# Softmax sums of two attention layers: turned and added up by VectorE, quadrants summed by 16-column products

## The chip, the cores and the metric

One Trainium2 chip, one core of it. The time is the device time of one execution in microseconds (us), given as the median of several executions. Everything is float32; TensorE multiplies it in two passes per product, except where operands are declared float32r ("fp32r"), which takes one.

## The reference

Two residual layers over x of shape (8, 32, 32, 512): a batch of 8 images, 1024 positions each (32 x 32), 512 channels. gn is a group norm over 32 groups of channels without weights.

```python
# layer 0: 16 heads of 32
q, k, v = split(gn(x) @ w_qkv)                 # w_qkv 512 x 1536
attn = softmax(q @ k.T * 32 ** -0.5)           # per image and head 1024 x 1024
x = x + (attn @ v) @ w_proj + b_proj
# layer 1: 4 heads of 128, with logits of relative position
q, k, v = gn(x) @ Wq * 128 ** -0.5, gn(x) @ Wk, gn(x) @ Wv
attn = softmax(q @ k.T + rel_w(q) + rel_h(q))
x = x + (attn @ v) @ Wo
```

A softmax is an exponential divided by the sum of the exponentials over the 1024 keys. How that sum is formed is what the change is about: 8 images x 16 heads x 1024 queries of them in layer 0, 8 x 4 x 1024 in layer 1.

## The kernel before

**Layout.** The program is unrolled over the 8 images ("batches"). Activations lie transposed, channels on the 128 partitions, positions along the row. Attention computes the transposed scores: 128 keys on the partitions, 512 queries along the row, so a query's sum runs over the partitions and over 8 key blocks. No maximum is subtracted; every sum is instead checked (L665 writes the maximum of sum + 1/sum), and at the end one product with ones (L1296) carries the verdict to a flag, on which the general path would run instead. It does not run here.

**Projections.** Each of the eight (512 x 512 matrices) is done in halves of seven products of half-size blocks, from sums of input blocks (forming, L343, additions at L370, written f_xn, f_ao and so on) and prepared sums of weights. `by_columns` (L327) issues a product as four 32-column strips (L331). Seven (about L407) takes three banks of PSUM, x, y and z, from `bank`, a pool of three 2 KB banks under one tag, and VectorE adds up y and p1 into snapshots a (L421) and b (L429), each before TensorE may go on adding to y. The name says which projection: y_wo and a_wo belong to the output projection of layer 1, y_q to a query projection.

**Attention of layer 0** (`attention_0`, from L685): 64 steps a batch over (m, h, j): m is one of 4 groups of four heads, h one of 2 halves of the queries, j one of 8 key blocks. A group is the 8 steps of one (m, h), so there are 8 groups a batch. `front` (L690): products of keys and queries into the four-bank tile ps (L698, eight products of 64 keys per step), one exponential over 128 x 2048 (L713) into one of three buffers of e_room. `back`, for the step before: value products into the bank "acc" (L724), and VectorE's addition of the exponentials into the group's sum esum, 128 x 2048 (L736, seven a group). At a group's last step ScalarE copies acc into q (L739), the undivided output. `finish`, called before the next step's front: four products with a 128 x 32 block of ones and esum, one per head, into the same bank "acc" (L746): each head's 32 partitions then hold its sums, repeated. `normalise` (L651): a copy to SBUF by ScalarE (L657), a 32 x 32 block transpose by VectorE (L659), so that 16 columns hold the sums once, reciprocal (L662), check (L665), transpose back with broadcast (L675), multiplication into q by GpSimd (POOL, L679).

**Attention of layer 1** (`attention_1`, from L811): 4 heads x 2 halves x 8 key blocks, again 64 steps and 8 groups a batch. `front`: keys and queries (L821), position logits (L822) into a bank, exponential of 128 x 512 (L824). `back`: value products (L833), VectorE's additions into es (L842, L844), a copy (L847). `finish` is a generator, of which a part runs per step: esum is split into its fp32r part (cast by ScalarE, L861) and the rest (subtraction on VectorE, L863), two steps later two one-pass products with 128 x 128 ones (L869, L870) go into a bank of ps, then normalise. Only three groups of the last batch (`beside`), which run next to first-layer attention, use one fp32 product with ones (L854) into `bank` instead. The very last group has VectorE do the final multiplication.

**What sets the order.** `side_by_side` (L1138) interleaves the 64 steps of attention_0 of batch b with everything else that is ready: output projection of layer 0 of batch b-1 (after_0), output projection of layer 1 of batch b-2 with its output transposes (after_1, put_out, L1098) and the group norm of batch b-1 (group_norm, L265; norm_1), then second (query, key, value projections of layer 1 and position logits, posT, L802, L807), attention_1, and the projections of batch b+1. Each part yields its cost; attention_1 yields 0 in all but the last batch, so it runs as one block of about 125 us in each period of about 470 us, and attention_0 of the batch stands still in that time. Within that program order a scheduler places each engine's instructions by its own estimate; `issue_after` and `keep_in_program_order` are further constraints. Each engine then runs its own queue in order; semaphores between the queues are the only other order.

Of the kernel before, what the change touches and what calls it, by code (L numbers as in the profile page):

```python
# [9 lines left out]
F32 = mybir.dt.float32  # L10
# [17 lines left out]
def quick_path(  # L28
# [52 lines left out]
    def bank(name, shape=None):  # L81
        return psum.tile(shape or [P, NB], F32, tag="bank", name=name, bufs=3)
# [1 line left out]

    ident = consts.tile([P, P], F32, tag="ident", name="ident")
    make_identity(nc, ident)
    ones_r = consts.tile([P, P], F32R, tag="ones", name="ones")
    nc.gpsimd.memset(ones_r.bitcast(F32), 1.0)
    ones = ones_r.bitcast(F32)
    bproj_sb = consts.tile([P, CC], F32, tag="bproj_sb", name="bproj_sb")  # L90
    with nc.allow_non_contiguous_dma(reason="512 values, once"):
        nc.gpsimd.dma_start(bproj_sb, b_proj.rearrange("(cc p) -> p cc", p=P))
# [5 lines left out]
    neg_half = consts.tile([P, CC], F32, tag="neg_half", name="neg_half")  # L98
    nc.gpsimd.memset(neg_half, -0.5)


    sel = consts.tile([P, IH, IW], F32R, tag="sel", name="sel")

    def fill_sel():
        for u in range(4):
            rows = slice(32 * u, 32 * u + 32)
            eye = ident[rows, rows]
            eye = eye.unsqueeze(2) if u % 2 else eye.unsqueeze(1)
            nc.vector.tensor_copy(sel[rows], eye.to_broadcast([32, IH, IW]))
# [541 lines left out]
    def normalise(dst, acc_sums, name, engine=nc.gpsimd):  # L651

        su = mem.tile([P, NB], F32, tag="rec", name=f"su_{name}", bufs=2)
        nc.scalar.copy(su, acc_sums)  # L657
        turned = mem.tile([P, NB], F32, tag="rec", name=f"tu_{name}", bufs=2)
        nc.vector.transpose(turned, su)  # L659
        few = turned.rearrange("p (t c) -> p t c", c=32)[:, :, 0]  # L660
        rec = mem.tile([P, NB // 32], F32, tag="few", name=f"rc_{name}", bufs=2)
        nc.vector.reciprocal(rec, few)  # L662
        at = check_at[0]
        check_at[0] += 1
        nc.vector.tensor_tensor_reduce(  # L665
            out=few,
            in0=few,
            in1=rec,
            op0=ALU.add,
            op1=ALU.max,  # L670
            scale=1.0,
            scalar=0.0,
            accum_out=checks[:, at : at + 1],
        )
        nc.vector.transpose(  # L675
            su.rearrange("p (t c) -> p t c", c=32),
            rec.unsqueeze(2).to_broadcast([P, NB // 32, 32]),
        )
        engine.tensor_tensor(dst, dst, su, op=ALU.mult)  # L679
# [5 lines left out]
    def attention_0(q, k, v, b, blocks=range(NT)):  # L685
# [55 lines left out]

        def finish(m, h, esum):
            name = f"0_{b}_{m}_{h}"
            su = psum.tile([P, NB], F32, tag="acc", name=f"sums_{name}", bufs=1)
            for r in range(HB):
                nc.tensor.matmul(  # L746
                    su[r * D0 : (r + 1) * D0, :],
                    ones[:, :D0],
                    esum[:, r, :],
                    start=True,  # L750
                    stop=True,
                )
            normalise(q[m][:, h * NB : (h + 1) * NB], su, name)

        pending = None
        for at in steps:
            if "ended" in state:
                finish(*state.pop("ended"))
            e = front(*at)
            if pending is not None:  # L760
                back(*pending)
            pending = (*at, e)
            yield 2
        back(*pending)
        yield 1
        finish(*state.pop("ended"))

    def position_logits(q, posT, b):

# [41 lines left out]
    def attention_1(q, k, v, posT, b, beside=0):  # L811
# [37 lines left out]

        def finish(h, c, esum):  # L850
            name = f"1_{b}_{h}_{c}"
            if (h * NH + c + 1) * NT < beside:
                su = bank(f"sums_{name}")
                nc.tensor.matmul(su, ones, esum, start=True, stop=True)  # L854
                normalise(q[:, h, c * NB : (c + 1) * NB], su, name)
                return

            yield

            greater = mem.tile([P, NB], F32R, tag="rec", name=f"sg_{name}", bufs=2)  # L860
            nc.scalar.copy(greater, esum)  # L861
            rest = mem.tile([P, NB], F32R, tag="rec", name=f"sr_{name}", bufs=2)
            nc.vector.tensor_sub(rest, esum, greater.bitcast(F32))  # L863

            yield
            yield

            su = psum.tile([P, HB, NB], F32, tag="ps", name=f"sums_{name}", bufs=1)[:, 0, :]
            nc.tensor.matmul(su, ones_r, greater, start=True, stop=False)  # L869
            nc.tensor.matmul(su, ones_r, rest, start=False, stop=True)  # L870

            end = (b, h, c) == (B - 1, H1 - 1, NH - 1)
            normalise(
                q[:, h, c * NB : (c + 1) * NB], su, name, nc.vector if end else nc.gpsimd
            )

# [257 lines left out]
    def run(part):  # L1134
        for _ in part:
            pass
# [65 lines left out]
    WV0.add_up([nc.gpsimd] * 2 + [nc.vector] * 2, nc.gpsimd, keep=True)  # L1202
    WQ0.add_up([nc.vector] * 4, nc.gpsimd, keep=True)
    fill_sel()
    stream = Stream(plan)

    def key_sums():
# [84 lines left out]
    nc.vector.tensor_reduce(worst, checks, axis=AX.X, op=ALU.max)  # L1292
    bad = small.tile([P, 1], F32, tag="bad", name="bad")
    nc.vector.tensor_scalar(bad, worst, SUM_BOUND, None, op0=ALU.is_gt)
    pf = bank("pf", [P, 1])
    nc.tensor.matmul(pf, ones, bad, start=True, stop=True)  # L1296
    nc.vector.tensor_copy(flag, pf)


def both_paths(tc: tile.TileContext, *args: bass.AP):  # L1300
# [480 lines left out]
```

## Time and profile before

| | |
|---|---|
| median of 3 runs | 3814.26 us (3814.05 to 3816.88) |
| span of the profiled execution | 3815.0 us |
| granted TensorE clock, mean | 0.998 of full speed |
| TensorE busy | 3786.7 us (99%), weight loads beside it 1376.4 us |
| VectorE busy | 2574.9 us (67%) |
| ScalarE busy | 1761.8 us (46%) |
| GpSimd busy | 660.0 us (17%) |
| DMA | 234.74 MB, 62 GB/s in the mean |

The span, from the first instruction to the last, is the only time that the profiled execution has of its own; it lies 0.7 us above the median of the runs. PE is TensorE's multiplication, PEld its weight load, which may run beside a multiplication; DVE is VectorE, ACT ScalarE, POOL GpSimd, SP the engine that issues most DMAs. L746 is line 746 of the kernel.

In a list of groups, "x512 | 71.3, 597 | 2.5 <-ACT q L739 2.0" means 512 instructions, 71.3 us of busy time that no other counts twice, 597 ns from start to end of one, and 2.5 us for which the engine stood idle just before them, 2.0 of them until ScalarE's instruction at L739 had ended. Tiles are written out<-in, with partitions x elements. Products of 512 columns overlap in the records (a new one starts before the end of the last is modelled), so starts are the better measure. In a timeline the first two numbers are start and duration, "x8" counts neighbours put together, and brackets hold the idle time before and what ended it. In a table of windows each row gives length, then busy time and count of PE, PEld, DVE, ACT and POOL, then the clock, the DMA share and GB/s.

### The profile page before, as it was taken

To read this page: it belongs to the slowest core of one execution; us is meant where nothing else is said; L and a number is where in the kernel's file an instruction comes from. 1 tells how busy PE (TensorE), PEld (TensorE's weight loads), DVE (VectorE), ACT (ScalarE), POOL (GpSimd) and SP (SyncE) were. 2 spreads that over 40 slices of the span, in tenths; PEclk is the share of its full clock that TensorE was granted. 3 is DMA by queue.
4 is the path that set the end of the run, shared out by engine and by line. 5 is a ranking of instruction groups with operands and counts; after the bars stand their busy time and mean duration, and the time that the engine had idled before them with its cause. 6 is when DMAs were issued, how large, how long until landed. Compare 5 with 4: busy or idle time off the path is not lost. (4 is left out here: it accounts for less than half of the span.)

```text
span 3815.0 us, 79937 instructions
## 1 busy us (share of the span) xinstructions
PE 3786.7 (99%) x34478; PEld 1376.4 (36%) x34478; DVE 2574.9 (67%) x2967; ACT 1761.8 (46%) x1830; POOL 660.0 (17%) x397
## 2 busy tenths in 40 slices
PE   9999999999999999999999999999999999999998
PEld 4232244323443234432343323433234332334353
DVE  6778665586656866569665686656866569665545
ACT  2555544445444454444544445444454445553132
POOL 1342101131101310013111131111310113001201
PEclk9999999999999999999999999999999999999999
DMA  6132120232202312034120241103411033110321
GB/s 186 62 105 70 39 56 10 71 102 53 56 12 92 86 46 56 16 93 93 38 53 19 94 95 40 45 23 98 91 41 40 26 98 77 33 37 31 110 41 26
DMA packets 482985, 234.74 MB, mean 62 GB/s; under 512 B 269600, under 2 KB 461376, under 8 KB 481600
## 3 DMA queue, kind: packets, MB, share of 16 engines
q1 hardware_dynamic: 470992, 213.74, 20.8%
q0 software_dynamic: 2608, 13.70, 1.0%
q8 instruction: 274, 4.49, 0.5%
q10 hardware_dynamic: 9024, 2.10, 0.3%
q14 instruction: 87, 0.71, 0.1%
HBM read 170.72 MB, written 58.72 MB: 60 GB/s over the span
## 5 line engine op out<-in xcount | busy, mean ns | idle before, releaser
L736 DVE TENSOR_TENSOR e_room<-e_room 128x2048 f32<-128x2048 f32 x448 | 1078.6, 2407 | 396.4 <-ACT e_room L713 393.7
L713 ACT ACTIVATE e_room<-ps 128x2048 f32<-128x2048 f32 x512 | 961.8, 1879 | 788.5 <-PE ps L698 744.2
L698 PE MATMUL ps<-q,k 32*64 32x512 f32 x8192 | 577.7, 613 | 0.2 <-ACT e_room L713 0.2
L724 PE MATMUL acc<-e_room,v 128*32 128x512 f32 x4096 | 545.8, 604 | 0.0
L824 ACT ACTIVATE e<-ps 128x512 f32<-128x512 f32 x512 | 305.7, 597 | 507.4 <-PE ps L822 436.3
L821 PE MATMUL ps<-q,k 128*128 128x512 f32 x1024 | 525.0, 594 | 0.2 <-DVE posT L807 0.2
L833 PE MATMUL acc<-e,v 128*128 128x512 f32 x1024 | 522.0, 593 | 0.3 <-ACT e L824 0.3
L679 POOL TENSOR_TENSOR q<-q,su 128x512 f32<-128x512 f32 x127 | 198.2, 1560 | 1524.8 <-DVE su L675 1423.5
L844 DVE TENSOR_TENSOR es<-es,e 128x512 f32<-128x512 f32 x384 | 290.5, 757 | 250.9 <-ACT e L824 248.3
L822 PE MATMUL ps<-posT,sel 128*128 128x512 f32 x512 | 406.6, 794 | 0.0
L821 PEld LDWEIGHTS ps<-q,k 128*128 128x128 f32 x1024 | 192.6, 190 | 230.1 <-issue 218.5
L698 PEld LDWEIGHTS ps<-q,k 32*64 32x64 f32 x8192 | 120.4, 129 | 391.3 <-issue 223.1
L833 PEld LDWEIGHTS acc<-e,v 128*128 128x128 f32 x1024 | 193.1, 189 | 147.3 <-issue 92.6
L724 PEld LDWEIGHTS acc<-e_room,v 128*32 128x32 f32 x4096 | 81.3, 108 | 411.4 <-issue 364.1
L659 DVE STREAM_TRANSPOSE tu<-su 128x512 f32<-128x512 f32 x128 | 90.6, 708 | 98.2 <-ACT su L657 96.5
L822 PEld LDWEIGHTS ps<-posT,sel 128*128 128x128 f32 x512 | 97.3, 190 | 122.5 <-issue 122.5
L657 ACT COPY su<-sums 128x512 f32<-128x512 f32 x128 | 74.9, 585 | 131.1 <-PE sums L746 81.3
L807 DVE TENSOR_TENSOR posT<-pp,posT 32x512 fp32r<-32x512 f32 x128 | 112.0, 875 | 32.2 <-ACT posT L802 30.9
L583 POOL TENSOR_TENSOR k<-b_k,p_k 128x512 f32<-128x512 f32 x32 | 50.7, 1584 | 477.7 <-ACT p_k L435 467.0
L802 ACT CAST posT<-pp 32x512 fp32r<-32x512 f32 x128 | 106.1, 829 | 46.0 <-PE pp L789 44.9
L583 POOL TENSOR_TENSOR v<-b_v,p_v 128x512 f32<-128x512 f32 x32 | 51.5, 1611 | 436.5 <-ACT p_v L435 436.5
L583 POOL TENSOR_TENSOR q<-b_q,p_q 128x512 f32<-128x512 f32 x32 | 67.9, 2121 | 255.2 <-ACT p_q L435 255.2
(223 smaller groups left out, 4542.3 us busy)
## 6 DMA issues: line engine op xcount, KB each, us to landing
w_qkv<-ws_qkv SPq DMA_DIRECT2D x168, 128.0 KB, 2.5
d<-x0T SPq DMA_DIRECT2D x32, 512.0 KB, 3.2
x1T<-d SPq DMA_DIRECT2D x32, 512.0 KB, 5.7
d<-x1T SPq DMA_DIRECT2D x32, 512.0 KB, 3.6
x2T<-d SPq DMA_DIRECT2D x32, 512.0 KB, 6.2
w_qkv<-in_L_conv_w_qkv SPq DMA_DIRECT2D x126, 128.0 KB, 2.2
out<-ot SPq DMA_DIRECT2D x240, 64.0 KB, 2.0
xs<-in_x SPq DMA_DIRECT2D x224, 64.0 KB, 2.5
```

The lines of the kernel that those rows point to most:

```text
L583: nc.gpsimd.tensor_tensor(self.dst[1][1], s(b), s(p7), op=ALU.add)
L679: engine.tensor_tensor(dst, dst, su, op=ALU.mult)
L698: nc.tensor.matmul(ps[some, r, :], k[m][rows, j * P + 64 * i : j * P + 64 * i + 64], q[m][rows, h * NB : (h + 1) * NB], start=True, stop=True,
L713: nc.scalar.activation(e, ps, AF.Exp, scale=D0 ** -0.5)
L724: nc.tensor.matmul(acc[r * D0 : (r + 1) * D0, :], v[:, j, c0 : c0 + D0], e[:, r, :], start=(j == blocks[0]), stop=(j == blocks[-1]),)
L736: summed[0] = nc.vector.tensor_add(state["esum"], state["esum"], e)
L807: nc.vector.tensor_sub(rest, logits, greater)
L821: nc.tensor.matmul(ps, k[h][:, keys], q[:, h, queries], start=True, stop=False)
L822: nc.tensor.matmul(ps, sel_flat[:, keys], posT[:, h, queries], start=False, stop=True)
L824: nc.scalar.activation(e, ps, AF.Exp, scale=1.0 / math.sqrt(D1))
L833: nc.tensor.matmul(acc, v[:, j, h * D1 : (h + 1) * D1], e, start=(j == 0), stop=(j == NT - 1),)
L844: added[0] = nc.vector.tensor_add(state["esum"], state["esum"], e)
```

## The change

The sums over the 128 partitions are formed in another way. `added_up` transposes the sum tile of 128 x 512 in 32 x 32 blocks on VectorE and reduces each block along its row: of 512 columns 16 remain, and partition 32g + i, column t, holds the sum over the 32 keys of quadrant g for query 32t + i. What is left is to add four quadrants. A product does this whose weights are 32 x 32 unit matrices stacked (`fold`, [128, 4, 32], filled by `fill_fold` on VectorE), and whose moving operand has those 16 columns. Its result is, in 16 columns, what the transpose L659 made before, so that ScalarE's copy and that transpose go, and reciprocal and check read PSUM (`normalise_few`). The transpose back and the multiplication stay.

In layer 0 `finish` becomes a generator, called after `back` instead of before `front`. Two of a group's four transposes and reductions are issued in the step in which the group ends, two in the step after, together with the four 16-column products (one per head, 32 columns of weights), which go into a tile of `bank` instead of "acc". A batch's last group keeps the four products with ones in "acc" and `normalise` as before. In layer 1 `added_up` stands for cast and subtraction, and two steps later a single fp32 product with all 128 columns of fold for the two fp32r products, into the same bank of ps, or, in the three groups beside first-layer attention, into `bank` as before. The ones become [128, 32], and the final flag product writes 32 rows.

```diff
--- before.py
+++ after.py
@@ -84,9 +84,8 @@
 
     ident = consts.tile([P, P], F32, tag="ident", name="ident")
     make_identity(nc, ident)
-    ones_r = consts.tile([P, P], F32R, tag="ones", name="ones")
-    nc.gpsimd.memset(ones_r.bitcast(F32), 1.0)
-    ones = ones_r.bitcast(F32)
+    ones = consts.tile([P, D0], F32, tag="ones", name="ones")
+    nc.gpsimd.memset(ones, 1.0)
     bproj_sb = consts.tile([P, CC], F32, tag="bproj_sb", name="bproj_sb")
     with nc.allow_non_contiguous_dma(reason="512 values, once"):
         nc.gpsimd.dma_start(bproj_sb, b_proj.rearrange("(cc p) -> p cc", p=P))
@@ -98,6 +97,17 @@
     neg_half = consts.tile([P, CC], F32, tag="neg_half", name="neg_half")
     nc.gpsimd.memset(neg_half, -0.5)
 
+
+
+    fold = consts.tile([P, P // 32, 32], F32, tag="fold", name="fold")
+    fold_flat = fold.rearrange("p g i -> p (g i)")
+
+    def fill_fold():
+        nc.vector.tensor_reduce(
+            fold[:, 0, :], ident.rearrange("p (a i) -> p i a", i=32), axis=AX.X, op=ALU.add
+        )
+        for g in range(1, P // 32):
+            nc.vector.tensor_copy(fold[:, g, :], fold[:, 0, :])
 
     sel = consts.tile([P, IH, IW], F32R, tag="sel", name="sel")
 
@@ -658,12 +668,31 @@
         turned = mem.tile([P, NB], F32, tag="rec", name=f"tu_{name}", bufs=2)
         nc.vector.transpose(turned, su)
         few = turned.rearrange("p (t c) -> p t c", c=32)[:, :, 0]
-        rec = mem.tile([P, NB // 32], F32, tag="few", name=f"rc_{name}", bufs=2)
+        multiply(dst, few, few, su, name, engine)
+
+    def added_up(out, esum, name):
+
+        turned = mem.tile([P, NB], F32, tag="rec", name=f"tu_{name}", bufs=2)
+        nc.vector.transpose(turned, esum)
+        nc.vector.tensor_reduce(
+            out, turned.rearrange("p (t c) -> p t c", c=32), axis=AX.X, op=ALU.add
+        )
+
+    def few_tile(name, n=1):
+        return mem.tile([P, n, NB // 32], F32, tag=f"few{n}", name=name, bufs=3 if n == 1 else 1)
+
+    def normalise_few(dst, few, name, engine=nc.gpsimd):
+        su = mem.tile([P, NB], F32, tag="rec", name=f"su_{name}", bufs=2)
+        multiply(dst, few, few_tile(f"sp_{name}")[:, 0, :], su, name, engine)
+
+    def multiply(dst, few, spare, su, name, engine):
+
+        rec = few_tile(f"rc_{name}")[:, 0, :]
         nc.vector.reciprocal(rec, few)
         at = check_at[0]
         check_at[0] += 1
         nc.vector.tensor_tensor_reduce(
-            out=few,
+            out=spare,
             in0=few,
             in1=rec,
             op0=ALU.add,
@@ -741,29 +770,41 @@
 
         def finish(m, h, esum):
             name = f"0_{b}_{m}_{h}"
-            su = psum.tile([P, NB], F32, tag="acc", name=f"sums_{name}", bufs=1)
+            dst = q[m][:, h * NB : (h + 1) * NB]
+            if (m, h) == steps[-1][:2]:
+                su = psum.tile([P, NB], F32, tag="acc", name=f"sums_{name}", bufs=1)
+                for r in range(HB):
+                    nc.tensor.matmul(
+                        su[r * D0 : (r + 1) * D0, :], ones, esum[:, r, :], start=True, stop=True
+                    )
+                normalise(dst, su, name)
+                return
+            few = few_tile(f"fw_{name}", HB)
+            for r in range(HB):
+                added_up(few[:, r, :], esum[:, r, :], f"{name}_{r}")
+                if r % 2:
+                    yield
+            su = bank(f"sums_{name}")[:, : NB // 32]
             for r in range(HB):
                 nc.tensor.matmul(
-                    su[r * D0 : (r + 1) * D0, :],
-                    ones[:, :D0],
-                    esum[:, r, :],
-                    start=True,
-                    stop=True,
+                    su[r * D0 : (r + 1) * D0, :], fold[:, 0, :], few[:, r, :], start=True, stop=True
                 )
-            normalise(q[m][:, h * NB : (h + 1) * NB], su, name)
+            normalise_few(dst, su, name)
 
         pending = None
+        ending = iter(())
         for at in steps:
-            if "ended" in state:
-                finish(*state.pop("ended"))
             e = front(*at)
             if pending is not None:
                 back(*pending)
             pending = (*at, e)
+            if "ended" in state:
+                ending = finish(*state.pop("ended"))
+            next(ending, None)
             yield 2
         back(*pending)
         yield 1
-        finish(*state.pop("ended"))
+        run(finish(*state.pop("ended")))
 
     def position_logits(q, posT, b):
 
@@ -849,28 +890,24 @@
 
         def finish(h, c, esum):
             name = f"1_{b}_{h}_{c}"
-            if (h * NH + c + 1) * NT < beside:
-                su = bank(f"sums_{name}")
-                nc.tensor.matmul(su, ones, esum, start=True, stop=True)
-                normalise(q[:, h, c * NB : (c + 1) * NB], su, name)
-                return
-
+            aside = (h * NH + c + 1) * NT < beside
             yield
 
-            greater = mem.tile([P, NB], F32R, tag="rec", name=f"sg_{name}", bufs=2)
-            nc.scalar.copy(greater, esum)
-            rest = mem.tile([P, NB], F32R, tag="rec", name=f"sr_{name}", bufs=2)
-            nc.vector.tensor_sub(rest, esum, greater.bitcast(F32))
+            few = few_tile(f"fw_{name}")[:, 0, :]
+            added_up(few, esum, name)
 
             yield
             yield
 
-            su = psum.tile([P, HB, NB], F32, tag="ps", name=f"sums_{name}", bufs=1)[:, 0, :]
-            nc.tensor.matmul(su, ones_r, greater, start=True, stop=False)
-            nc.tensor.matmul(su, ones_r, rest, start=False, stop=True)
+            if aside:
+                su = bank(f"sums_{name}")
+            else:
+                su = psum.tile([P, HB, NB], F32, tag="ps", name=f"sums_{name}", bufs=1)[:, 0, :]
+            su = su[:, : NB // 32]
+            nc.tensor.matmul(su, fold_flat, few, start=True, stop=True)
 
             end = (b, h, c) == (B - 1, H1 - 1, NH - 1)
-            normalise(
+            normalise_few(
                 q[:, h, c * NB : (c + 1) * NB], su, name, nc.vector if end else nc.gpsimd
             )
 
@@ -1202,6 +1239,7 @@
     WV0.add_up([nc.gpsimd] * 2 + [nc.vector] * 2, nc.gpsimd, keep=True)
     WQ0.add_up([nc.vector] * 4, nc.gpsimd, keep=True)
     fill_sel()
+    fill_fold()
     stream = Stream(plan)
 
     def key_sums():
@@ -1292,9 +1330,9 @@
     nc.vector.tensor_reduce(worst, checks, axis=AX.X, op=ALU.max)
     bad = small.tile([P, 1], F32, tag="bad", name="bad")
     nc.vector.tensor_scalar(bad, worst, SUM_BOUND, None, op0=ALU.is_gt)
-    pf = bank("pf", [P, 1])
+    pf = bank("pf", [P, 1])[:D0]
     nc.tensor.matmul(pf, ones, bad, start=True, stop=True)
-    nc.vector.tensor_copy(flag, pf)
+    nc.vector.tensor_copy(flag[:D0], pf)
 
 
 def both_paths(tc: tile.TileContext, *args: bass.AP):
```

## Prediction

> **What bounds the kernel now.** I read the page's busy times and slices first, then the groups, then TensorE's instructions in order of time around the sums, then busy time by windows, then VectorE's instructions in its fullest stretch.
>
> ```profile
> span 3815.0 us, 79937 instructions
> PE 3786.7 (99%) x34478; PEld 1376.4 (36%) x34478; DVE 2574.9 (67%) x2967; ACT 1761.8 (46%) x1830; POOL 660.0 (17%) x397
> ```
>
> TensorE is the bound, and not only by its modelled busy time. Products of 512 columns follow one another every 0.43 us per pass (four column strips at once), two passes each, nearly without holes, so a product removed is time removed, as long as nothing new makes TensorE wait. VectorE has a third of the span free on average.
>
> The work that goes and the work beside it, from the groups:
>
> ```profile
> L736 DVE TENSOR_TENSOR e_room<-e_room 128x2048 f32<-128x2048 f32 x448 | 1078.6, 2407 | 396.4 <-ACT e_room L713 393.7
> L659 DVE STREAM_TRANSPOSE tu<-su 128x512 f32<-128x512 f32 x128 | 90.6, 708 | 98.2 <-ACT su L657 96.5 <-POOL q L679 1.5
> L746 PE MATMUL sums<-e_room,ones 128*32 128x512 f32 x512 | 71.3, 597 | 2.5 <-ACT q L739 2.0 <-DVE e_room L736 0.4
> L869 PE MATMUL sums<-sg,ones 128*128 128x512 f32 x61 | 46.3, 758 | 0.0
> L870 PE MATMUL sums<-sr,ones 128*128 128x512 f32 x61 | 24.4, 400 | 0.0
> ```
>
> These durations overlap their neighbours. What a group really takes is read from starts in the timeline:
>
> ```profile
> 1746.84 1.05 PE L746 MATMUL sums<-e_room,ones 128*32 128x512 f32 x8
> 1747.82 1.11 PE L698 MATMUL ps<-q,k 32*64 32x512 f32 x16
> ```
>
> ```profile
> 2043.74 1.02 PE L833 MATMUL acc<-e,v 128*128 128x512 f32 x2
> 2044.20 0.80 PE L869 MATMUL sums<-sg,ones 128*128 128x512 f32 x1
> 2044.83 0.40 PE L870 MATMUL sums<-sr,ones 128*128 128x512 f32 x1
> 2045.07 1.02 PE L821 MATMUL ps<-q,k 128*128 128x512 f32 x2
> ```
>
> A first-layer slot is 1747.82-1746.84 = 0.98 us, of which some 0.12 us (0.98 less two passes of 0.43) is the change of tile shape to L698, which stays. So 0.86 us goes. In the second layer L833's two passes end at about 2043.74+0.86 = 2044.60, and the next product starts at 2045.07: 0.47 us.
>
> VectorE is not idle everywhere. By windows (the columns are PE, PEld, DVE, ACT, POOL):
>
> ```profile
> 1750.00:1770.00 20.00, 20.00 (x212) 5.14 (x208) 19.04 (x30) 8.51 (x7) 12.15 (x6) 1.00 0.47 138
> 1770.00:1790.00 20.00, 20.00 (x212) 5.12 (x208) 19.90 (x20) 10.45 (x9) 7.79 (x3) 1.00 0.52 94
> 1810.00:1830.00 20.00, 20.00 (x212) 5.03 (x208) 11.82 (x13) 10.33 (x9) 1.28 (x1) 1.00 0.26 59
> ```
>
> For some 65 us of each period of 470 us (group norm, output transposes and the output projection beside attention) it is full. There it already runs late, with little to spare:
>
> ```profile
> 1772.98 1.88 ACT L713 ACTIVATE e_room<-ps 128x2048 f32<-128x2048 f32 x1 [0.50 <-PE ps L698]
> 1777.87 0.69 DVE L421 TENSOR_TENSOR a_wo<-y_wo,p_wo 128x512 f32<-128x512 f32 x1
> 1778.47 2.28 DVE L736 TENSOR_TENSOR e_room<-e_room 128x2048 f32<-128x2048 f32 x1
> 1779.15 1.90 PE L331 MATMUL y_wo<-f_ao,w_o 128*32 128x512 f32 x16
> ```
>
> The exponential ended at 1774.86 and its addition began at 1778.47, 3.6 us late; and the snapshot a_wo ended at 1778.56, 0.6 us before the product that overwrites y_wo. Elsewhere the addition starts within 0.03 us of its exponential and VectorE waits:
>
> ```profile
> 1818.46 2.29 DVE L736 TENSOR_TENSOR e_room<-e_room 128x2048 f32<-128x2048 f32 x1 [1.47 <-ACT e_room L713]
> 1820.67 0.68 DVE L421 TENSOR_TENSOR a_q<-y_q,p_q 128x512 f32<-128x512 f32 x1
> 1824.70 0.69 DVE L429 TENSOR_TENSOR b_q<-y_q,p_q 128x512 f32<-128x512 f32 x1 [3.35 <-PE y_q L331]
> ```
>
> **What the Trainium skill says.** "VectorE: DVE Perf Modes", perf-mode tier table and Specifications: a reduction runs at one element per cycle at 0.96 GHz, as fp32 additions do. The trace agrees for the addition (2048 elements in 2.29 us); it has only 32-element reductions (L271, 0.18 us). "TensorE: Matmul & The Clock Gate", LDWEIGHTS: a weight load takes columns/1.2 ns, so 107 ns for 128 and 27 for 32. The final flag product agrees: two passes of one column behind 128-column loads took
>
> ```profile
> 3799.36 0.30 PEld L1296 LDWEIGHTS pf<-bad,ones 128*128 128x128 f32 x2 [0.84 <-issue]
> ```
>
> 0.30 us with 0.19 for one, so the loads stood 0.11 us apart. "TensorEngine Tiling (Array Packing)", Key Properties: tiles load and multiply in parallel, but a new tiling mode drains the engine; the 0.12 us above fits. "TensorE: Matmul & The Clock Gate", Architectural detail: VectorE and ScalarE run strictly in order; so a burst on VectorE holds up whatever is queued behind it.
>
> **The change part by part.**
>
> *First layer, TensorE.* 56 of 64 groups (seven a batch) lose 0.86 us and get four 16-column products, two passes each, in the tile shape of their new neighbours L724 and L331 (no drain). Two rounds of four parallel strips, each behind a 27 ns load: between 0.05 us (all hidden) and 0.26 us (loads in series, 8x27 ns, and some issue). I take 0.12: 56 x 0.74 = 41 us. The waits ahead of L746 (page: 2.5 us idle) go too: 3 us.
>
> *Second layer, TensorE.* 61 groups lose 0.47 us and 3 lose 0.86 us (L854). One 16-column product with 128-column weights comes in: two exposed loads of 0.11 to 0.13 us. I take 0.26 (bounds 0.15 and 0.45, at which almost nothing is left): 61 x 0.21 + 3 x 0.6 = 15 us.
>
> *ScalarE* loses 120 copies L657 (0.585 us) and 61 casts L861 (0.62): 108 us. It is no bound at 46%; nothing is credited but the last group's chain, which loses a cast, a copy and two handovers and gets a reduction for the subtraction: 1 us at the end of the kernel, where TensorE waits for VectorE.
>
> *Second layer, VectorE.* L863 (0.69) and L659 (0.71) go, a transpose (0.71) and a 512-element reduction come: no change. The reciprocal and the check now read PSUM and hold that bank until VectorE gets there; the bank is one of L698's four, unused during second-layer attention. The few constants of fill_fold run while TensorE waits for its first data: nothing, at most 0.5 us without that cover.
>
> *First layer, VectorE.* Four transposes and four reductions per group. Back to back a transpose costs 0.62 us; a reduction of 512 elements is 512/0.96 = 0.53 us and up to the 0.69 us of an equally long addition; I take 0.61. 8 x 0.61 = 4.9 us, less the old transpose and its wait (0.65): 4.3 us a group, 56 x 4.3 = 240 us. It does not change TensorE's work, so its price is the waiting it causes. In a quiet stretch the group's last addition (1818.46) is followed by 8 us in which VectorE now does three short operations and sits idle about 5 us; the next addition is not due in the following step. So 4.9 us fit: nothing.
>
> In the full stretch two groups a period end (L746 at 1746.84 and again near 1792). Behind the first burst are queued the last statistics, a_wo and the next addition, all about 3.4 us later than now. The first place where TensorE feels it strongly is a_wo at 1777.87: 3.1 us later (two idle moments of 0.3 us give some back) against 0.6 us of slack, so TensorE stands 2.5 us behind its present place at 1779.15. The second burst follows the f_xn sum (in the built program four more operations stand between its pieces) and ends at about 1797.5; the new products wait for it in TensorE's queue where it would arrive at 1792.1+0.9 less the 0.86 saved plus the 2.5 behind, 1794.5. TensorE ends 1797.7-1793.0 = 4.7 us behind its present timeline, the two groups' own savings included; without them 6.2 us of waiting. Five periods: 31 us. Batch 1 has one such group (4 us). In the last batch the same stretch already stalls TensorE by 1.7 us (additions 5.9 us late), so nearly all of two bursts counts: 8 us. Batch 0 steps every 3.3 to 3.8 us with additions of up to 3.2 us; its reciprocals stand ahead of the next addition and wait for the new products: 0.5 us a group, 3.5 us.
>
> *Banks.* The sums leave the accumulator's bank, so the next group no longer waits for L657, and take one of the three banks of the projections until VectorE has read them. In quiet stretches they are read about 1 us later; a projection's new bank is asked for some 1.7 us (one product) later. Zero, at worst 0.3 us x 43 quiet groups = 13 us.
>
> Sum: 41+3+15+1 = 60 us off, 31+4+8+3.5 = 46.5 us on: 13.5 us less. The profiled span of 3815.0 us becomes 3801.5; the median of the runs lies 0.7 below that span: **3801**.
>
> **The rivals.** (1) *The bursts hide*: VectorE's full stretch has slack in work nobody waits for (output transposes, norm), waits cost below 15 us. For it: 33% of VectorE is idle and additions have 5 us of slack outside. Against: it runs in order. 60-12: 3766. (2) *Even*: waits of about 58 us eat the gain; 3812. It needs reductions of 0.7 us (0.8 us more a group) and bank waits of 0.15 us. (3) *TensorE waits for each group's sums*: the 16-column products stand at a fixed place in TensorE's queue, two steps after the group, and the whole queue stands behind them. If the bursts arrive late there in quiet stretches too, because snapshots, additions or posT pieces come between, the waits add 1.2 us in each of the 43 quiet groups, 52 us: 3853 at most, 3833 with half of that and wider bank waits. It decides from 60/56 = 1.1 us of waiting a group. Against it: 3.3 us idle at 1824.70. (4) *Second-layer loads not shorter than what went*: 15 us less gain, 3815, counted within (2).
>
> **How the numbers follow.** Forecast (3785 to 3807) 0.45, (1) 0.13, (2) 0.17, (3) 0.25. The range leaves out the tips of (1) and (3): 3764 to 3834. Faster by over 0.2% (about what a measurement of this kernel tells from no change: below 3806.6) 0.54, within 0.2% 0.20, slower 0.26.
>
> **What would show it.** The timeline: new products of about 0.12 and 0.26 us from start to next start; reductions of 0.6 to 0.7 us; VectorE near 2800 us busy. Waits for the reductions at the new first-layer products, only in two groups a period near the norm; a_wo late there by 3 us. Wrong if such waits stand in most groups (3), if projections wait for a bank, or if no wait shows at all (1).

## The result and the profile after

The changed kernel takes 3838.14 us (median of 4 runs, 3832.24 to 3839.4), the kernel before 3814.16 in the same comparison: ratio 1.0058, 95% interval 1.0044 to 1.0072. It is slower by 24 us, where 3801 had been forecast, and lies 4 us above the range.

The first lines of the page of the kernel after:

```profile
span 3837.4 us, 80059 instructions
PE 3750.1 (98%) x34478; PEld 1362.3 (35%) x34478; DVE 2768.3 (72%) x3366; ACT 1656.4 (43%) x1649; POOL 699.0 (18%) x397
```

TensorE's busy time fell by 36.6 us and its idle time grew by 59. VectorE works 193 us more, close to what was expected (2800 busy). So the work went where it was meant to go, and the loss is waiting. The new groups, with shapes kept apart:

```profile
L677 DVE TENSOR_REDUCE fw<-tu 128x16 f32<-128x512 f32 x288 | 182.9, 664 | 2.2
L676 DVE STREAM_TRANSPOSE tu<-e_room 128x512 f32<-128x512 f32 x224 | 145.3, 684 | 2.1 <-POOL q L708 1.7
L907 PE MATMUL sums<-fw,fold 128*128 128x16 f32 x128 | 19.5, 227 | 0.0
L789 PE MATMUL sums<-fw,fold 128*32 128x16 f32 x448 | 19.3, 184 | 23.2 <-DVE fw L677 21.3 <-DVE posT L848 1.6
```

L727 is now the first layer's product of keys and queries, L753 its values, L765 the addition, L341 the projections, L789 the first layer's 16-column products, L907 the second layer's. A quiet stretch of the timeline shows all that was priced:

```profile
1854.33 1.24 DVE L677 TENSOR_REDUCE fw<-tu 128x16 f32<-128x512 f32 x2
1855.48 1.29 DVE L676 STREAM_TRANSPOSE tu<-e_room 128x512 f32<-128x512 f32 x2
1856.70 1.24 DVE L677 TENSOR_REDUCE fw<-tu 128x16 f32<-128x512 f32 x2
1857.86 0.68 DVE L439 TENSOR_TENSOR b_q<-y_q,p_q 128x512 f32<-128x512 f32 x1
1859.53 2.29 DVE L765 TENSOR_TENSOR e_room<-e_room 128x2048 f32<-128x2048 f32 x1 [0.99 <-ACT e_room L742]
1863.80 0.23 PE L789 MATMUL sums<-fw,fold 128*32 128x16 f32 x8
1863.86 1.90 PE L341 MATMUL z_q<-x1T,w_q 128*32 128x512 f32 x16
```

The six operations from 1854.33 to 1857.86 take 0.59 us each in a row (0.61 and 0.62 were taken), the next addition still waits for its exponential, and the eight passes of L789 cost 1863.86-1863.80 = 0.06 us of TensorE (0.12 was taken). They stand two steps after the group's end, because the generator pauses after each pair of reductions; the section on the change puts them one step too early.

What TensorE waits for, in the kernel after (in total, times, longest):

```profile
PE sums L789 <- DVE fw L677: 21.3, 23, 2.2
PE y_wo L341 <- DVE a_wo L431: 7.4, 10, 0.9
PE y_q L341 <- DVE b_q L439: 4.8, 2, 4.0
PE acc L874 <- DVE checks L694: 4.8, 5, 1.0
PE y_q L341 <- DVE a_q L431: 4.1, 6, 1.8
PE y_q L341 <- DVE x2T L608: 4.1, 4, 1.4
PE z_k L341 <- issue: 3.2, 1, 3.2
PE z_v L341 <- issue: 3.2, 1, 3.2
PE y_k L341 <- DVE a_k L431: 2.7, 1, 2.7
```

**Where.** Each kernel has the same 512 steps of attention in each layer. The lag is the start of a step's first product of keys and queries minus the start of the same one before the change. Its growth, from the traces (batch 0 means from its first step to batch 1's; the first column is what lies ahead of that; the last ends at the span's end):

| us | ahead | batch 0 | batch 1 | batches 2 to 6 | rest | span |
|---|---|---|---|---|---|---|
| terms of the prediction | 0 | -2 | -3 | -5 | -3 | -13.5 |
| after | -1.8 | +15.3 | +9.8 | +4.3 | -5.2 | +22.4 |

The 20 quiet first-layer groups of batches 2 to 6 whose sums fall among projections gain 0.7 to 0.8 us each, and a second-layer group gains 0.25. The five periods in the middle come out 2 us each above the forecast in the mean, 3.3 at most (batch 3). 30 us of the 36 us between forecast and span are made in the first two batches, where the prediction saw a gain of 5 us.

**The middle, mostly as foreseen.** In the full stretch of batch 4:

```profile
1807.21 1.92 PE L341 MATMUL y_wo<-f_ao,w_o 128*32 128x512 f32 x16 [0.94 <-DVE a_wo L431]
1821.64 0.24 PE L789 MATMUL sums<-fw,fold 128*32 128x16 f32 x2 [1.20 <-DVE fw L677]
1822.83 0.20 PE L789 MATMUL sums<-fw,fold 128*32 128x16 f32 x1 [0.95 <-DVE fw L677]
1826.23 1.92 PE L341 MATMUL y_q<-f_xn,w_q 128*32 128x512 f32 x16 [1.43 <-DVE x2T L608]
```

Snapshot a_wo is late behind the first burst, the new products wait for the second one, and then y_q waits for its bank, which the output's additions (L608) still read. The wait at a_wo is shorter than the 2.5 us forecast, and the one for a bank was not forecast here.

**Batch 1, not foreseen.** First the kernel after, then the same place before:

```profile
454.68 3.45 DVE L848 TENSOR_TENSOR posT<-pp,posT 32x512 fp32r<-32x512 f32 x4 [0.94 <-ACT posT L843]
454.84 0.23 PE L789 MATMUL sums<-fw,fold 128*32 128x16 f32 x8
458.16 0.26 DVE L691 RECIPROCAL rc<-sums 128x16 f32<-128x16 f32 x1
458.23 3.11 PE L341 MATMUL z_k<-x1T,w_k 128*32 128x512 f32 x16 [3.16 <-issue]
461.04 2.53 PE L341 MATMUL y_k<-f_xn,w_k 128*32 128x512 f32 x16
```

```profile
436.77 3.54 DVE L807 TENSOR_TENSOR posT<-pp,posT 32x512 fp32r<-32x512 f32 x4 [0.93 <-ACT posT L802]
436.93 1.90 PE L331 MATMUL z_k<-x1T,w_k 128*32 128x512 f32 x16
438.65 1.90 PE L331 MATMUL y_k<-f_xn,w_k 128*32 128x512 f32 x16
```

The pool has three banks. y_k, the position logits pp and z_k filled them before; the sums are a fourth. z_k starts 0.1 us after L848 has read pp (454.68+3.45 = 458.13), so it was given pp's bank, presumably because the sums held the other one.

And z_k then takes 461.04-458.23 = 2.81 us instead of 1.72. Windows of the kernel after there (us, busy times of five engines, granted clock):

```profile
455.00:458.20 3.20, 0.07 (x11) 0.00 (x0) 3.13 (x5) 1.55 (x1) 0.00 (x0) 1.00 0.00 0
458.20:461.00 2.80, 2.77 (x16) 0.89 (x20) 2.77 (x5) 0.00 (x0) 1.60 (x1) 0.61 0.02 6
461.00:463.50 2.50, 2.50 (x21) 0.71 (x13) 0.43 (x1) 0.58 (x1) 2.50 (x2) 0.75 0.18 52
```

The granted clock falls to 0.5 for 3.4 us after the wait. The Trainium skill tells this in "TensorE: Matmul & The Clock Gate", section "What's actually happening": TensorE's clock is halved after an idle window of about 3.4 us, and the window runs freely. Between the first step of attention and the last 10 us the trace has eight stretches at half clock, of 3.41 or 6.83 us. They begin 64, 22, 14, 110, 138, 275 and 273 times 3.413 us after one another, so it agrees that the windows run freely. It does not agree that a window must be idle: seven of the eight stretches follow waits shorter than 3.4 us, like the one of 3.16 us here. The stretches last 34 us in all, so up to 17 us of the loss are slow products and not waits. The kernel before has none there. The prediction used that page for weight loads and for VectorE's order, and overlooked this.

**Batch 0, not foreseen.** After, then before:

```profile
158.34 6.09 DVE L765 TENSOR_TENSOR e_room<-e_room 128x2048 f32<-128x2048 f32 x1 [1.49 <-ACT e_room L742]
164.35 0.68 DVE L439 TENSOR_TENSOR b_q<-y_q,p_q 128x512 f32<-128x512 f32 x1
165.08 3.46 PE L341 MATMUL y_q<-f_xn,w_qkv 128*32 128x512 f32 x10 [4.01 <-DVE b_q L439]
170.47 0.19 PE L789 MATMUL sums<-fw,fold 128*32 128x16 f32 x2
170.48 0.62 PE L341 MATMUL z_q<-x0T,w_qkv 128*32 128x512 f32 x2
```

```profile
155.08 1.04 PE L331 MATMUL z_q<-x0T,w_qkv 128*32 128x512 f32 x8
156.93 0.68 DVE L429 TENSOR_TENSOR b_q<-y_q,p_q 128x512 f32<-128x512 f32 x1
158.83 1.04 PE L331 MATMUL y_q<-f_xn,w_qkv 128*32 128x512 f32 x8
```

Before, TensorE worked on z_q while VectorE made the snapshot b_q. Now z_q, whose bank is asked for after that of the sums, stands behind the sums in TensorE's queue; y_q comes first and meets a snapshot that is not ready, with nothing to cover it. The 4.01 us are an extreme, though: the addition ahead of the snapshot took 6.09 us here, while no addition of the kernel before takes over 3.4. In the run that copies the sums out (below) none does either, and this wait is 0.96 us; batch 0 loses 14.9 us all the same.

### The profile page after: what moved, and what is told of

The parts are those of the page before. It is cut to its first block, busy times and chain, and to the rows that moved or that the text cites. A ratio compares the mean times of both kernels' runs of the same rounds, so it can differ in the third digit from the quotient of the medians.

```text
span 3837.4 us, 80059 instructions
## 1 busy us (share of the span) xinstructions
PE 3750.1 (98%) x34478; PEld 1362.3 (35%) x34478; DVE 2768.3 (72%) x3366; ACT 1656.4 (43%) x1649; POOL 699.0 (18%) x397
## 4 chain that ended last, share of the span: by engine, by line
PE 83%; DVE 12%; issue 2%; ACT 1%; DMA 1%; POOL 1%; SPq 0%; DVEq 0%; POOLq 0%; ACTq 0%
PE acc L874 12%; PE ps L862 11%; PE ps L727 11%; PE acc L753 10%; PE y_v L341 4%; PE y_k L341 4%; PE y_q L341 4%; DVE e_room L765 4%; PE ps L863 3%; PE z_k L341 3%; PE z_q L341 3%; PE x_v L341 3%; PE x_k L341 3%; PE z_v L341 3%; PE x_q L341 2%
## 5 line engine op out<-in xcount | busy, mean ns | idle before, releaser
L765 DVE TENSOR_TENSOR e_room<-e_room 128x2048 f32<-128x2048 f32 x448 | 1042.9, 2328 | 382.8 <-ACT e_room L742 380.1
L727 PE MATMUL ps<-q,k 32*64 32x512 f32 x8192 | 575.6, 616 | 0.4 <-ACT e_room L742 0.4
L753 PE MATMUL acc<-e_room,v 128*32 128x512 f32 x4096 | 551.7, 604 | 0.0
L708 POOL TENSOR_TENSOR q<-q,su 128x512 f32<-128x512 f32 x127 | 262.0, 2063 | 1362.3 <-DVE su L704 1314.5
L885 DVE TENSOR_TENSOR es<-es,e 128x512 f32<-128x512 f32 x384 | 300.3, 782 | 289.3 <-ACT e L865 285.0
L727 PEld LDWEIGHTS ps<-q,k 32*64 32x64 f32 x8192 | 120.0, 130 | 386.7 <-issue 205.6
L753 PEld LDWEIGHTS acc<-e_room,v 128*32 128x32 f32 x4096 | 82.1, 108 | 413.6 <-issue 400.3
L677 DVE TENSOR_REDUCE fw<-tu 128x16 f32<-128x512 f32 x288 | 182.9, 664 | 2.2
L676 DVE STREAM_TRANSPOSE tu<-e_room 128x512 f32<-128x512 f32 x224 | 145.3, 684 | 2.1 <-POOL q L708 1.7
L593 POOL TENSOR_TENSOR q<-b_q,p_q 128x512 f32<-128x512 f32 x32 | 58.0, 1813 | 442.8 <-ACT p_q L445 419.3
L848 DVE TENSOR_TENSOR posT<-pp,posT 32x512 fp32r<-32x512 f32 x128 | 111.8, 873 | 31.6 <-ACT posT L843 30.3
```

The lines of the kernel that those rows point to most:

```text
L677: nc.vector.tensor_reduce(out, turned.rearrange("p (t c) -> p t c", c=32), axis=AX.X, op=ALU.add)
L727: nc.tensor.matmul(ps[some, r, :], k[m][rows, j * P + 64 * i : j * P + 64 * i + 64], q[m][rows, h * NB : (h + 1) * NB], start=True, stop=True,
L753: nc.tensor.matmul(acc[r * D0 : (r + 1) * D0, :], v[:, j, c0 : c0 + D0], e[:, r, :], start=(j == blocks[0]), stop=(j == blocks[-1]),)
L765: summed[0] = nc.vector.tensor_add(state["esum"], state["esum"], e)
L885: added[0] = nc.vector.tensor_add(state["esum"], state["esum"], e)
```

## The experiments

Two theories. *Lateness*: VectorE's bursts delay everything behind them, wherever the sums stand. *Place*: the loss of batches 0 and 1 comes from the sums' place in TensorE's queue and in the pool of banks, in front of the next projection's bank. Each kernel has 4 to 21 runs, and the kernel before 7 to 30 runs beside them. The comments in the code cuts are added here.

**The parts alone and by region.** In the first, third and fourth, a condition decides which first-layer groups are turned; the others keep ones, acc and the old place:

```diff
+        def turned_up(m, h):
+            return (m, h) != steps[-1][:2] and (False)      # third: b > 1; fourth: b > 1 and m > 0
...
-            if (m, h) == steps[-1][:2]:
+            if not turned_up(m, h):
...
         for at in steps:
+            if "ended" in state and not turned_up(*state["ended"][:2]):
+                run(finish(*state.pop("ended")))
             e = front(*at)
...
-            if "ended" in state:
+            if "ended" in state and turned_up(*state["ended"][:2]):
                 ending = finish(*state.pop("ended"))
```

In the second run the second layer's finish is the old one.

> Layer 1 alone is changed; all first-layer groups keep the four products with ones in their old place. The lag between the two traces falls by 0.25 us in each of the 64 second-layer groups of the changed kernel. If these savings are independent of layer 0: 64 x 0.25 = 16 us less, 3798. If VectorE's new work in layer 1 is felt elsewhere, less than 10 us: above 3804.

Measured 3793.55, ratio 0.9943 (0.9929 to 0.9956).

> Layer 0 alone is changed; layer 1 keeps cast, subtraction and two fp32r products. If the parts add up: 3838 + 16 = 3854, so the whole loss, and more, is layer 0's. If layer 1's part contributes to the loss: below 3845.

Measured 3858.81, ratio 1.0107 (1.0092 to 1.0123). The parts nearly add up: -21 and +44 make +23, for +24. The second layer's part is a gain without a loss, 5 us more of it than expected.

> Both layers changed, but the first-layer groups of batches 0 and 1 keep ones in their old place. In the changed kernel these two batches lose about 25 us against before, the later ones together about nothing. If the loss is local to those batches: 3838 - 26 = 3812. If it is caused by the bursts everywhere and only shows there first, the later batches take it over: above 3825.

Measured 3809.84, ratio 0.9988 (0.9982 to 0.9995). The loss of batches 0 and 1 is local to them.

> As the run that keeps ones in batches 0 and 1, and besides the first two groups of every later batch (m = 0), which end in VectorE's full stretch, keep ones. These two groups cost 5.8 to 7.5 us net a batch in the changed kernel, 37 us in six batches. If the full stretch is where the later batches' waits are made: 3812 - 37 = 3775. If the waits only move on to the next groups: about 3800.

Measured 3774.16, ratio 0.9892 (0.9877 to 0.9908). Two groups a batch make all the waits of the later batches, and these don't move on.

**Burst and place apart, first try.** The one keeps ones and issues reductions that nobody reads; the other issues the old products at the new place:

```diff
+            if "ended" in state and state["ended"][:2] != steps[-1][:2]:
+                ending = reductions(*state["ended"])   # four added_up, two a step; finish: ones, as before
```

```diff
-            few = few_tile(f"fw_{name}", HB)
-            for r in range(HB):
-                added_up(few[:, r, :], esum[:, r, :], f"{name}_{r}")
-                if r % 2:
-                    yield
-            su = bank(f"sums_{name}")[:, : NB // 32]
+            yield
+            yield
+            su = bank(f"sums_{name}")
...
-                    su[r * D0 : (r + 1) * D0, :], fold[:, 0, :], few[:, r, :], start=True, stop=True
+                    su[r * D0 : (r + 1) * D0, :], ones, esum[:, r, :], start=True, stop=True
...
-            normalise_few(dst, su, name)
+            normalise(dst, su, name)
```

> Layer 0 keeps the products with ones in their old place and bank in every group; the four transposes and reductions of 56 groups are issued where the change puts them, into a tile that nobody reads, so VectorE has the burst (and the old transpose besides), TensorE no new wait for it, and no bank is taken. Layer 1 changed. If VectorE's lateness alone makes the loss (snapshots, additions): about 50 of the 83 us of waits remain (without those at the new products and for banks): 3798 + 50 = 3848. If the sums' place among the projection banks makes it: about 3803 to 3815.

Measured 3889.15, ratio 1.0195 (1.0181 to 1.0209).

> Layer 0: no transposes and reductions; the four products with ones, of 512 columns, stand at the changed kernel's place in the program (a step later than before) and in its bank of the projections' three, read by ScalarE's old copy; batch's last group as before. Layer 1 changed. If the sums' place among the projection banks makes the loss (a projection's next bank stands behind them): 3798 + 25 = 3823 or more, most of it in batches 0 and 1. If VectorE's lateness alone makes it: 3796 to 3800. If it takes both together, this run and the one with the burst alone stay each below 3810.

Measured 3834.49, ratio 1.0054 (1.004 to 1.0068). Neither is clean. With the burst alone, TensorE waits most for something that the change doesn't have, the old copy of the sums, which itself waits 47.6 us for a reduction L677 (13 times) to free its SBUF buffer:

```profile
PE acc L753 <- ACT su L667: 23.9, 13, 3.0
PE y_q L341 <- DVE a_q L431: 18.6, 8, 3.3
PE ps L727 <- ACT e_room L742: 16.8, 11, 8.7
```

In the other run the products stand a step after the exponential that reuses the group's buffer: they read its new content, so the first layer's sums are of other data, and wait 14.0 us for it. The pair decides nothing.

**Burst and place apart, second try.** The 16-column products read a constant, once without and once with the burst:

```diff
-                    su[r * D0 : (r + 1) * D0, :], fold[:, 0, :], few[:, r, :], start=True, stop=True
+                    su[r * D0 : (r + 1) * D0, :], fold[:, 0, :], ones[:, : NB // 32], start=True, stop=True
```

> The changed kernel without the transposes and reductions of layer 0: the 16-column products stand at the same place and in the same bank, but read a constant (so the first layer's sums are left out); reciprocal, check, transpose back and multiplication stay. TensorE's savings are 56 x 0.80 + 64 x 0.25 = 61 us: 3753 is what is left if nothing waits. If the burst makes all waits: 3751 to 3757. If the sums' place among the projections' banks costs by itself in batches 0 and 1, as the run with 512-column products there suggests: 3762 to 3770, with the difference in these two batches.

Measured 3762.81, ratio 0.9862 (0.9847 to 0.9877). z_k and z_v wait 3.2 us each here too, with half clock after them; the lag jumps by 5.1 and 4.8 us there. So the place costs 10 us by itself, in batch 1, and the 75 us that lie between this run and the change need the burst.

> The changed kernel with its burst on VectorE, but the 16-column products of layer 0 read a constant instead of the reduced tile (the sums are left out), so TensorE doesn't wait for the burst there; 23 us of such waits are in the changed kernel's trace. If they are a loss of their own: 3838 - 21 = 3817. If VectorE's next late piece (snapshots, additions) takes their place: above 3828.

Measured 3818.46, ratio 1.0011 (1.0004 to 1.0017). The 20 us that go are nearly all in batch 0: its lag falls by 5.2 instead of growing by 15.3. In batches 2 to 6 the waits at L789 are gone, but the lag grows as before; y_q, behind them, now waits for its bank:

```profile
PE y_q L341 <- DVE x2T L608: 17.2, 6, 3.3
```

**The sums' place.** First only the bank is given back sooner:

```diff
-            normalise_few(dst, su, name)
+            got = few_tile(f"gt_{name}")[:, 0, :]
+            nc.scalar.copy(got, su)
+            normalise_few(dst, got, name)
```

> The changed kernel, but ScalarE copies the 16 columns of a first-layer group's sums out of the bank, so it is given back without VectorE. If banks held for VectorE's late reading are a main cost (z_k and z_v waited 3.2 us each in batch 1, y_q about 1.4 us in later batches): 10 to 15 us less, 3825. If not: 3836 to 3840.

Measured 3833.53, ratio 1.0053 (1.0039 to 1.0066), between the two. In batch 1 the jumps at z_k and z_v remain (5.1 and 4.8 us of lag): a quicker reader doesn't help z, which seems to have its bank from the order of requests.

Then the place itself:

```diff
+    def behind_y():
+        while waiting:
+            waiting.pop()()
...
         sink.early(p1, a)              # seven, behind the first product into y
+        behind_y()
...
-            su = bank(f"sums_{name}")[:, : NB // 32]
...
+            waiting.append(sums)       # the bank, the four products, normalise_few
+            for _ in range(3):
+                yield
+            behind_y()
```

> The changed kernel, with the 16-column products and their bank asked for right behind the first product into y of the running projection (three steps later at most), where two projection banks are in use and the next is asked for four products later; so no z stands behind the sums, and the burst has up to three steps more. If the place among the banks is half of the loss in batches 0 and 1: 3838 - 12 = 3826, and below 3820 if the waits at the products of the full stretch go too. If only VectorE's lateness counts, felt at the snapshots: 3835 to 3840.

Measured 3805.34, ratio 0.9975 (0.9966 to 0.9985): 33 us better than the change, by asking for one bank, and issuing four small products, at another point. The growth of the lag in all runs that decide:

| us | ahead | batch 0 | batch 1 | batches 2 to 6 | rest | span |
|---|---|---|---|---|---|---|
| after | -1.8 | +15.3 | +9.8 | +4.3 | -5.2 | +22.4 |
| layer 1 alone | -1.3 | +0.1 | -2.7 | -10.4 | -8.9 | -23.2 |
| no burst | -1.9 | -7.2 | +4.3 | -36.0 | -12.9 | -53.7 |
| free products | -1.5 | -5.2 | +6.6 | +5.6 | -6.1 | -0.5 |
| anchored | -1.4 | -4.5 | -1.2 | +2.2 | -6.5 | -11.4 |
| quiet groups | -1.5 | 0.0 | -2.6 | -26.7 | -11.7 | -42.5 |
| anchored, quiet | -2.2 | -4.4 | -4.7 | -33.0 | -12.8 | -57.1 |

Batch 0's loss needs products that wait for the burst: without the burst, or with products that don't read its result, it gains. It also gains when the products are anchored, but anchoring does two things: no z stands behind the sums, and the burst gets up to three steps more. The waits at the products fall from 8.1 to 3.4 us in batch 0. Which of the two counts there is not shown.

Batch 1 loses 10 us by the place: both jumps are there without the burst, and gone when anchored. It also loses by lateness, behind its one group in the full stretch (y_k waits for a_k): there the lag grows by 4.6 us in the changed kernel, 4.5 with free products and 3.6 anchored, and not at all without the burst.

Batches 2 to 6 lose by lateness in the full stretch, wherever the sums stand.

The anchored run also shows the clock by itself. Windows over the 5.5 us that follow a wait of 3.23 us in batch 5 and one of 3.22 us in batch 6, at the same place in the program:

```profile
2236.50:2242.00 5.50, 5.50 (x44) 1.20 (x48) 5.47 (x10) 1.37 (x2) 2.02 (x1) 0.70 0.50 75
2705.60:2711.10 5.50, 5.48 (x56) 1.46 (x60) 5.47 (x10) 2.46 (x2) 2.01 (x1) 1.00 0.51 76
```

```profile
2236.50 3.56 PE L341 MATMUL x_wo<-q,w_o 128*32 128x512 f32 x16 [3.23 <-DVE x2T L615]
2239.99 1.11 PE L734 MATMUL ps<-q,k 32*64 32x512 f32 x16
...
2705.62 1.92 PE L341 MATMUL x_wo<-q,w_o 128*32 128x512 f32 x16 [3.22 <-DVE x2T L615]
2707.47 1.11 PE L734 MATMUL ps<-q,k 32*64 32x512 f32 x16
```

The same product takes 3.49 us after the one and 1.85 us after the other, and the lag over that group grows by 5.4 and 4.05 us. The same wait can cost 1.3 us more or not. The windows fit this: the run's six stretches at half clock begin whole multiples of 3.413 us apart, so that one window ends at 2236.43, just as the first wait ends, and another at 2704.05, in the middle of the second. The saving did not last: in batch 6 the clock fell 29 us later instead, at 2734.78, after a wait of 2.39 us, and the two periods end within 0.3 us of one another (0.4 and 0.7 us of lag).

**Better versions.** More quiet groups (in batch 1 those of m = 1 and 3, and the second of m = 0, are turned as well), then anchored and quiet together (turned: `m > 0 or b == 0 or (b == 1 and h == 1)`):

> As the run with quiet groups (3774.2), and in batch 1 the four groups turned in whose step range the changed kernel's trace gains about 0.8 to 1.1 us. If gains and losses are local to a group: 4 x 0.8 = 3 us less, 3771.

Measured 3770.48, ratio 0.9884 (0.9869 to 0.9899).

> The 16-column products anchored behind y, in all groups that are turned; ones kept in the first two groups of batches 2 to 7, in the first of batch 1 and in each batch's last. The anchored kernel's lag falls by 2 us over batch 0 and by 1 us more in batch 1 than that of the run with quiet groups, which had ones there: if the parts add up, 3774 - 2 - 4 x 0.8 - 0.6 = 3768. If anchoring costs the quiet groups something: 3774 or more.

Measured 3759.76, ratio 0.9857 (0.9841 to 0.9874): 55 us better than the kernel before, and 8 us better than expected, mostly because anchoring also helps the quiet groups' periods (6.6 us less lag a batch instead of 5.3). The largest of its waits that are not at the start:

```profile
PE sums L801 <- DVE fw L684: 3.4, 5, 1.5
PE z_wo L341 <- ACT p_wo L517: 0.8, 1, 0.8
```

## Why the prediction was wrong

- *First layer, TensorE*, 41 us and 3 of waits: right. 56 x 0.80 = 45 us, seen in the quiet groups; the run without burst, 52 us faster than before, holds it together with the second layer.
- *Second layer*, 15 us and 1 at the end: right in kind, a quarter too small. 0.25 instead of 0.21 us a group; the layer alone brings 21 us, 1.3 of them ahead of any attention and 8.9 in the last batch and after it.
- *VectorE's burst*: right in size (0.59 us an operation; 193 us in all, where 240 were forecast) and right that it is free in quiet stretches (0.80 us of gain a group stays).
- *The full stretch*, 31 us in five periods: right in kind and place. Measured by the run without the burst against that with free products, (36.0+5.6)/5 = 8.3 us a period instead of 6.2, 42 us. Part of the difference is the clock, which fell in three of these stretches. The one such group of batch 1: 4 us forecast, 3.6 to 4.6 measured. Batch 7 and the end: 8 forecast, 12.9-6.1 = 6.8 measured in the same way.
- *Batch 0*, 0.5 us a group, 3.5 us: failed. It is the term that was mis-sized most: about 20 us (15.3 - (-5.2) with free products). The step saw the reciprocals wait for TensorE; what counts is TensorE waiting for the reductions, 8.1 us at the products themselves, and what follows from it. That y_q lost its cover is seen in the trace; what it costs by itself is not measured.
- *Banks*, "Zero, at worst 0.3 us x 43 quiet groups": failed. It argued that a bank is asked for 1.7 us later in a quiet stretch. In batch 1 position logits hold a bank beside y, and z stood waiting: two jumps of 5 us. And the order in which a pool's banks are asked for seems to set TensorE's order as well, as z_q in batch 0 shows: this was not thought of at all.
- *Waits priced at their length*: failed. Those of over 3 us can cost up to 1.9 us more in slow products.
- The rival (3) named the mechanism, TensorE's queue behind the sums, and 3833. Its place was wrong: it expected it in the quiet groups of all batches; it was mostly in the first two batches.

Not tried: a fourth bank for the sums, beside four for ps, one for acc and three for the projections; and, for batch 0, an anchored place that gives the burst no more time than the change does.

## What to carry to other kernels

Where a queue runs in order and is nearly full, a small instruction that depends on a slower engine costs what stands behind it: look up what follows in the queue and which buffer of a shared pool it takes, and put it where the next request is far off (here, behind the first product into y). Move work to an engine stage by stage, where that engine is idle, and leave the old way where it is full; here 13 more of 64 groups so left turned a loss of 24 us into a gain of 55, together with the better place. And add the clock to the price of each long wait of TensorE.

## What the runs showed of the hardware

- Four 16-column fp32 products in four column strips, two passes each, take 0.06 us of TensorE between neighbours of the same tile shape (1863.80 to 1863.86 in the changed kernel).
- In the changed and in the anchored kernel, all stretches at half clock begin on one grid of 3.413 us. A wait of 3.2 us within one window of this grid halved the clock (anchored, batch 5); one of the same length that lay across two windows did not (batch 6). In batch 5 of the changed kernel it also fell, at 2291.8, after waits of only 1.19 and 0.95 us close together.
- Transposes of 128x512 fp32 and reductions of 512 elements run in turn at 0.59 us each on VectorE (six of them, 1854.33 to 1857.86 in the changed kernel).
